# First heads' q and k at the head of the opening, row maxima of two groups taken ahead of a branch

## The chip, the cores and the metric

The kernel runs on one core of one Trainium2 chip. The metric is device time in microseconds of one execution, as the median of the runs shown. The engines are named as the profile names them: PE (TensorE matmul), PEld (its weight loads), DVE (VectorE), ACT (ScalarE), POOL (GpSimd) and SP (SyncE, which here only issues DMAs). Each engine works through its own instructions in program order and waits on semaphores for the others.

## The reference, cut to what matters

A transformer layer in float32 on x of shape (16, 512, 512): attention with 32 heads of 16, rotary embedding and a causal mask, then a gated feed-forward layer whose weights take the values -1, 0 and 1, each inside a layer norm on both sides, with residuals.

```python
h = _layernorm(x)
q, k, v = (split_heads(h @ W.T + b) for W, b in ((Wq, bq), (Wk, bk), (Wv, bv)))
q, k = (apply_rope(apply_rope(t, freqs_abs), freqs_temp) for t in (q, k))
s = jnp.where(causal, einsum('bhqd,bhkd->bhqk', q, k) / sqrt(dh), -inf)
out = einsum('bhqk,bhkd->bhqd', softmax(s), v) @ Wo.T + bo
x = x + _layernorm(out)
f = _layernorm(x)                     # gate_w, up_w (1408, 512), down_w (512, 1408)
x = x + _layernorm(((silu(f @ gate_w.T * gate_s) * (f @ up_w.T * up_s)) @ down_w.T) * down_s)
```

## The kernel before, in words

**Tiles and batches.** The 16 sequences ("batches") are worked one after the other. A batch has 512 rows in four blocks of 128 (`NB`), 512 features in four chunks of 128 (`NC`), and its 32 heads form eight groups of four (`NG`). The products q, k, v and o are float32 matmuls of 128x128 by 128x512; four of them, one for each chunk, make a block.

**Attention in steps.** A group takes six steps (`STEPS`), a pair of its heads at a third of the score matrix at a time. In one step (`one_step`, line 792) TensorE computes transposed scores of group n into the PSUM tile `st` (with the row maximum subtracted by a matmul of `mx` with ones), ACT takes their exponential into `pt`, POOL masks the diagonal; and scores of the group that follows into two PSUM tiles `s`, of which DVE takes row maxima (`maxima`, line 607). Steps 0 and 1 of group n take the maxima of group n + 1's last third, steps 2 to 5 those of group n + 2's first two. After step 2 `turn_maxima` (line 617) transposes a group's maxima, splits them into a high and a low part (`nmh`, `nml`) and has SP put them into rows of `mx`. A group's operands come from DRAM (`load_group`, line 549): q, and the high and low part of k (`kh`, `kl`), 256 KB each, three buffers of each. The weighted values (`values`, `av`) follow in steps 3 and 0.

**Filling.** Beside a step, TensorE works on a list of other matmuls: the projections of the batch to come and the feed-forward layer of the batch before. `run_list` (line 696) cuts such a list into as many equal shares of its costs as there are steps (1 for a float32 matmul of 512 columns, 0.15 for a transpose) and gives out one share for a step, behind the step's scores. A list item can be the issue of a DMA, of cost 0. The first list (`first_list`, line 884) holds what is left of batch 1's v, its q and k blocks, the transposes of batch 2's input and a product that folds biases: 46.4 units of cost. It is given out over 56 steps: ten that only take maxima (of group 0, and of group 1 but for its last third), ahead of group 0's own, and 46 of batch 0's 48.

**The q and k blocks** (`qk_block`, line 329). After the four matmuls into a PSUM tile, ACT makes two rotated copies (`ys`), DVE multiplies the PSUM tile by the cosines (`ya`), POOL multiplies `ys` by the sines; then (`rest`) DVE adds them into `ya`, ACT rounds it to a high part `yh`, POOL subtracts for a low part `yl`; then (`store`) SP writes both to DRAM in four DMAs. `ya` and `ys` have one buffer, `yh` and `yl` two. Projections, transposes and turned maxima share three PSUM buffers, taken in turn.

**The opening** (`front`, line 808). It loads x of batches 0 and 1, normalizes and transposes them, and computes batch 0's q (four blocks), k (four blocks) and v (four), and batch 1's first two v blocks, in this order. Each block's `rest` and `store` come after the first two matmuls of the next q or k block. Between the blocks it checks the feed-forward weights (`check_weights`, line 196): a copy on ACT rounds a weight tile, a DVE instruction compares it with the tile and counts what differs; 11 gate/up tiles of 512 KB and 11 down tiles of 256 KB, gate/up first. A last matmul sums the counts into `flag`. `run` (line 929) reads the flag on every engine and branches: the exact arm uses the weights in a format of fewer bits, the other in float32. Each arm holds all sixteen batches (`batches`, line 951). The arm that the inputs lead to is the exact one. Tiles filled ahead of the branch aren't carried into an arm, save those in fixed buffers; q, k and batch 1's normalized x are taken from DRAM.

Line 49 of the profile is a helper that keeps instructions in program order (class `InOrder`); nearly all instructions have that line, so groups are told apart by tile names.

Of the kernel before, what the change touches and what calls it, by code (L numbers as in the profile page):

```python
# [10 lines left out]
FP = mybir.dt.float32  # L11
FR = mybir.dt.float32r
# [6 lines left out]
P = 128  # L19
T = 512  # L20
# [4 lines left out]
NB = T // P  # L25
# [28 lines left out]
class Block:  # L54
# [55 lines left out]
    def constants(self):  # L110
        nc, a, con = self.nc, self.a, self.const
        for tb in range(NB):
            self.load_x(0, tb, ("x", "xr")[tb // 2], 2)
        ncol = sum(n for _, n in a["cols"][1])
        cols = con.tile([P, ncol], FP, tag="cols", name="cols")
        self.sp.dma_start(out=cols, in_=a["cols"][0])
        self.col, at = {}, 0
        for name, n in a["cols"][1]:
            self.col[name] = cols[:, at : at + n]
            at += n  # L120
        turn = con.tile([P, 2, T], FP, tag="turn", name="turn")
        self.cos, self.sin = turn[:, 0, :], turn[:, 1, :]
        nc.scalar.dma_start(out=turn, in_=a["turn"])
        for half in range(2):
            self.load_w(0, "q", half)
        for tb in range(NB):
            self.load_x(1, tb, "x1", 4)
        for half in range(2):
            self.load_w(0, "k", half)
        self.ident = con.tile([P, P], FP, tag="ident", name="ident")  # L130
        make_identity(nc, self.ident)
        self.neghalf = con.tile([P, 1], FP, tag="neghalf", name="neghalf")
        nc.gpsimd.memset(self.neghalf, -0.5)
        self.row = {}
        for name in ("bo", "dscale"):
            self.row[name] = con.tile([P, C], FP, tag=name, name=name)
            nc.scalar.dma_start(out=self.row[name], in_=a[name].partition_broadcast(P))

        self.gh = con.tile([P, self.NF], FP, tag="gh", name="gh")
        self.gu = con.tile([P, self.NF], FP, tag="gu", name="gu")  # L140

        self.mask = con.tile([P, T], mybir.dt.bfloat16, tag="mask", name="mask")
        nc.gpsimd.memset(self.mask, 0.0)
        m = self.mask[:, T - P : T]
        nc.gpsimd.affine_select(
            out=m, in_=m, compare_op=ALU.is_ge, fill=-BIG, base=0, pattern=[[-1, P]], channel_multiplier=1
        )
        self.v17 = []
        for i in range(2):
            t = con.tile([P, NB, WIDTH], FP, tag=f"v17_{i}", name=f"v17_{i}")  # L150
            nc.gpsimd.memset(t, 0.0)
            nc.gpsimd.memset(t[:, :, DH : H * W : W], 1.0)
            self.v17.append(t)
        self.one = con.tile([P, P], FR, tag="one", name="one")
        nc.vector.memset(self.one.bitcast(FP), 1.0)
        self.qd, self.kd, self.od, self.rd = [], [], [], []
        for par in range(2):
            for c in range(NC):
                self.qd.append(self.dram.tile([P, 2, T], FP, tag=f"qd{par}{c}", name="qd"))
                self.kd.append(self.dram.tile([2, P, T], FP, tag=f"kd{par}{c}", name="kd"))  # L160
                self.od.append(self.dram.tile([8 * 32, T], FP, tag=f"od{par}{c}", name="od"))
                self.rd.append(self.dram.tile([8, T], FP, tag=f"rd{par}{c}", name="rd"))
        self.wgs = self.dram.tile([self.NF, P, 2, NC, P], FP, tag="wgs", name="wgs")
        self.wds = self.dram.tile([self.F, C], FP, tag="wds", name="wds")
        self.wd = con.tile([P, self.NF, C], FR, tag="wd", name="wd")
        self.xn1 = self.dram.tile([P, NC, T], FP, tag="xn1", name="xn1")
        self.odd = con.tile([P, 2 * self.NF], FP, tag="odd", name="odd")
        self.flag = con.tile([1, 1], mybir.dt.int32, tag="flag", name="flag")
        self.ones = con.tile([P, 1], FP, tag="ones", name="ones")
        nc.vector.memset(self.ones, 1.0)  # L170


    def load_checks(self):

        a, n = self.a, 2 * NC * P
        ht = self.tile([P, self.NF, T], "ht", bufs=1).rearrange("p f t -> p (f t)")
        xl = self.tile([P, NC, T], "xntfl", bufs=1).rearrange("p c t -> p (c t)")
        places = [ht[:, ts(i, n)] for i in range(self.NF * T // n)] + [xl[:, ts(i, n)] for i in range(NC * T // n)]
        small = [tag for tag, k in (("oc", 4), ("q2", 3), ("kh", 3), ("kl", 3)) for _ in range(k)]
        self.wgu0, self.wd0 = [], []  # L180

        def load(f):
            w = places.pop() if 3 <= f < self.NF - 1 else self.tile([P, n], "wf", bufs=3)
            self.sp.dma_start(out=w, in_=a["wgu"][f].rearrange("p w c j -> p (w c j)"))
            self.wgu0.append(w)

        for f in range(self.NF - 1):
            load(f)
        for f in range(self.NF):
            tag = small.pop()  # L190
            w = self.tile([P, C], tag, bufs=4 if tag == "oc" else 3)
            self.sp.dma_start(out=w, in_=a["wd"][ts(f, P), :])
            self.wd0.append(w)
        self.load_last = lambda: load(self.NF - 1)

    def check_weights(self):
# [20 lines left out]
            self.pe.matmul(p[0:1, 0:1], n, self.ones, start=True, stop=True)  # L217
            self.dve.tensor_copy(self.flag, p[0:1, 0:1])

        return [lambda f=f, g=g: g(f) for g in (gate_up, down) for f in range(self.NF)] + [total]  # L220

    def load_x(self, b, tb, tag="x", bufs=2):
        t = self.tile([P, C], tag, bufs=bufs)
# [338 lines left out]
    def scores(self, n, m, i):  # L562
# [4 lines left out]
        if 0 <= n < self.B * NG:  # L567
            ps = self.ps_t.tile([P, 2, T], FP, tag="st", name="st")
            q, ks, mx = self.qs[n], self.ks[n], self.mxs[n]
            for j in range(2):  # L570
# [3 lines left out]
                for kb, at, w in ST_SETS[third]:  # L574
# [3 lines left out]
                        (out, ks[1][r, ts(kb, P)], x, False, False),  # L578
                        (out, self.one[r2, :], mx[r2, T - w : T], False, True),
                    ]  # L580
        if 0 <= m < self.B * NG:
            if n < 0 and i % 2:
                both = self.ps_t.tile([P, 2, T], FP, tag="st", name="st")
                pm = [both[:, j, :] for j in range(2)]
# [29 lines left out]
                accum_out=self.nms[m][:, j, qb : qb + 1],  # L614
            )

    def turn_maxima(self, m):
        p = self.psum("pm")
        self.pe.transpose(p[0:16, 0:P], self.nms.pop(m).rearrange("p j b -> p (j b)"), self.ident)
        hi, lo = [self.tile([16, P], i, bufs=1, dtype=FR) for i in ("nmh", "nml")]  # L620
        self.act.copy(hi, p[0:16, 0:P])
        self.dve.tensor_tensor(lo, p[0:16, 0:P], hi, ALU.subtract)
        mx = self.mxs[m] = self.tile([P, T], "mx", bufs=2, dtype=FR)

        def put():
            for i, t in enumerate((hi, lo)):
                self.sp.dma_start(out=mx[i:P:32, :].bitcast(FP), in_=t.bitcast(FP))

        self.later(1, put)
# [162 lines left out]
    def one_step(self, work, n, i):  # L792
        for f, args in self.todo.pop(self.step, []):
            f(*args)
        if i == 0 and n + 2 < self.B * NG:
            self.load_group(n + 2)
        self.scores(n, n + 2 if i >= 2 else n + 1, i)
        if i == 2 and 0 <= n + 1 < self.B * NG:
            self.turn_maxima(n + 1)
        next(work, None)  # L800
        if i == 3 and 0 <= n < self.B * NG:
# [6 lines left out]
    def front(self):  # L808
# [5 lines left out]
        def check(n):  # L814
            for _ in range(min(n, len(checks) - 1)):
                checks.pop(0)()
# [24 lines left out]
            rest = now  # L841
        rest()
        turn(0, NB - 1)
        for k in range(2):
            r = [norm(1, 2 * k), norm(1, 2 * k + 1)]
            check(1)
            for f in r:
                f()
        rests = []
        for name in "qk":  # L850
            for c in range(NC):
                items, rest, store = self.qk_block(0, name, c)
                for _, f in items[:2]:
                    f()
                for f in rests:
                    f()
                for _, f in items[2:]:
                    f()
                rests = [rest, store]
                if name == "q" and c < 2:  # L860
                    for k in range(2):
                        turn(1, 2 * c + k)
                check(2)
            if name == "q":
                for half in range(2):
                    self.load_w(0, "v", half)
            else:
                self.sp.dma_start(out=self.xn1, in_=self.xnts["a", 1])
        for f in rests:
            f()  # L870
        check(len(checks))
        nc.vector.tensor_scalar_mul(self.gh, self.col["gs"], 0.5)
        nc.vector.tensor_tensor(self.gu, self.gh, self.col["us"], ALU.mult)
        for tb in range(NB):
            for _, f in self.v_block(0, tb):
                f()
            if tb == 2:
                checks.pop(0)()
        self.wts[1, "v", 0], self.wts[1, "v", 1] = self.wts[0, "v", 0], self.wts[0, "v", 1]
        for tb in range(2):  # L880
            for _, f in self.v_block(1, tb):
                f()

    def first_list(self):

# [64 lines left out]

    def batches(self):
        B = self.B
        work = self.run_list(self.first_list(), 56)
        self.load_group(0)
        for n, i0 in ((-2, 2), (-1, 0)):
            for i in range(i0, STEPS):
                self.one_step(work, n, i)
        for b in range(B):
            if b:
                if b < B - 1:  # L960
# [78 lines left out]
```

## Time and profile before

| | |
|---|---|
| runs (us) | 3213.71, 3211.56, 3219.57; median 3213.71 |
| profiled execution, its own time | 3215.86 us |
| its span | 3214.0 us |
| mean granted TensorE clock | 0.984 |
| busy: PE, DVE, ACT, POOL | 3097.9, 1888.0, 1542.7, 1383.9 us |
| first TensorE instruction | at 10.38 us |
| batch 0's first scores for weights | at 108.42 us |
| moved by DMA | 471.41 MB, 147 GB/s over the span |

Times within the span are in microseconds from its start. A row of the timeline gives start, duration, engine, line, operation, output tile, inputs, shapes and count, and in brackets how long the engine had been idle before it and what ended the wait. A float32 matmul of 512 columns appears as two records. A row of busy times by stretch gives the stretch and its length, then for PE, PEld, DVE, ACT and POOL the busy time with the number of instructions, and last the granted clock of TensorE (1.00 is full), the DMA engines' busy share and GB/s. A row of waits gives who waited for whom, the total, the number of times and the longest.

### The profile page before, as it was taken

How to read it: one execution, taken by the hardware profiler on the slowest of the kernel's cores; microseconds unless marked ns; L12 is line 12 of the kernel's file. 1: busy time of each engine (PE TensorE's matmuls, PEld its weight loads, DVE VectorE, ACT ScalarE, POOL GpSimd, SP SyncE). 2: the span in 40 equal slices, each digit the busy share in tenths (PEclk: the TensorE clock that was granted, in tenths of full speed). 3: DMA queues.
4: the chain of work that ended last, by engine and by line, in shares of the span. 5: the costliest groups of instructions: out<-in, count | busy, mean ns of one | idle time of the engine just before them, and what ended most of it. 6: DMA issues, size and time to landing. Idle time of an engine off the chain costs nothing.

```text
span 3214.0 us, 59287 instructions
## 1 busy us (share of the span) xinstructions
PE 3097.9 (96%) x21258; PEld 1743.3 (54%) x21258; DVE 1888.0 (59%) x5911; ACT 1542.7 (48%) x2243; POOL 1383.9 (43%) x1933
## 2 busy tenths in 40 slices
PE   6889999999999999999999999999999999999988
PEld 2334555646556464655646455464655646455556
DVE  5465656556565665656566565665656566565633
ACT  5354545454554544545454554544455454453432
POOL 4143445443544534345443544534345453443343
PEclk9899999999999999999999999999999999999999
DMA  6454534445353443525345352543535345343422
GB/s 251 166 166 152 189 101 163 139 149 172 108 190 106 160 164 123 195 93 177 127 152 173 127 185 96 168 147 123 195 101 183 122 147 172 123 156 105 131 97 71
DMA packets 227441, 471.41 MB, mean 147 GB/s; under 512 B 40976, under 2 KB 45072, under 8 KB 226704
## 3 DMA queue, kind: packets, MB, share of 16 engines
q1 hardware_dynamic: 226704, 466.47, 43.1%
q8 instruction: 170, 2.79, 0.4%
q10 hardware_dynamic: 432, 1.05, 0.1%
q14 instruction: 135, 1.11, 0.1%
HBM read 345.79 MB, written 125.30 MB: 147 GB/s over the span
## 4 chain that ended last, share of the span: by engine, by line
PE 83%; DVE 2%; DMA 2%; ACT 2%; POOL 1%; issue 1%; SPq 0%; ACTq 0%; DVEq 0%; POOLq 0%
PE st L49 16%; PE pu L49 11%; PE pg L49 10%; PE av L49 9%; PE pd L49 9%; PE po L49 7%; PE pq L49 6%; PE pv L49 5%; PE pk L49 5%; PE s L49 3%; DMA kl<-kd 2%; PE px L49 1%; ACT pt L49 1%; DVE s L49 1%; PE pm L49 1%
## 5 line engine op out<-in xcount | busy, mean ns | idle before, releaser
L49 DVE CUSTOM_DVE_ANT_0 s<-s,mask 128x512 f32<-128x512 f32 (+1 forms) x2034 | 974.9, 510 | 713.8 <-PE s L49 530.8
L49 ACT ACTIVATE pt<-st 128x1024 f32<-128x1024 f32 (+1 forms) x768 | 677.0, 882 | 755.9 <-PE st L49 746.9
L49 POOL TENSOR_SCALAR_AFFINE_SELECT pt<-pt 128x256 f32<-128x256 f32 (+1 forms) x768 | 393.8, 513 | 1202.3 <-ACT pt L49 1200.0
L49 PEld LDWEIGHTS st<-q,kh 32*128 32x128 f32 x2048 | 191.3, 183 | 463.3 <-issue 225.6
L49 PE MATMUL st<-q,kh 32*128 32x512 f32 (+3 forms) x2048 | 411.2, 398 | 22.3 <-ACT pt L49 20.9
L49 PE MATMUL s<-kh,q 32*128 32x512 f32 (+1 forms) x2034 | 411.6, 399 | 17.2 <-DVE nm L49 8.8
L49 PE MATMUL s<-kl,q 32*128 32x512 f32 (+1 forms) x2034 | 340.7, 321 | 11.2 <-DMA kl<-kd 11.2
L49 PE MATMUL av<-pt,v 128*32 128x512 f32 (+3 forms) x4096 | 336.0, 447 | 0.0
L49 PE MATMUL st<-q,kl 32*128 32x512 f32 (+3 forms) x2048 | 333.5, 322 | 0.0
L49 PE MATMUL st<-mx,one 2*128 2x512 f32 (+3 forms) x2048 | 333.0, 321 | 0.0
L49 POOL TENSOR_TENSOR hl<-ht,hh 128x512 fp32r<-128x512 f32 (+1 forms) x192 | 229.6, 1196 | 184.3 <-ACT hh L49 176.7
L49 PE MATMUL pd<-wd,hl 128*128 128x512 f32 x704 | 288.9, 410 | 9.2 <-POOL hl L49 9.2
L49 PE MATMUL pd<-wd,hh 128*128 128x512 f32 x704 | 290.9, 413 | 2.2 <-ACT hh L49 2.2
L49 DVE DVE_READ_ACCUMULATOR2_ANT nm<- 128x1 f32 x2048 | 288.8, 141 | 0.0
L49 PE MATMUL pg<-xntf,wf 128*128 128x512 f32 x704 | 287.4, 408 | 1.5 <-ACT xntf L49 1.5
L49 PE MATMUL pu<-xntfl,wf 128*128 128x512 f32 x704 | 284.3, 404 | 0.0
L49 PE MATMUL pu<-xntf,wf 128*128 128x512 f32 x704 | 283.9, 403 | 0.0
L49 PE MATMUL pg<-xntfl,wf 128*128 128x512 f32 x704 | 281.5, 400 | 0.6 <-DVE xntfl L49 0.6
L49 PE MATMUL po<-w,oc 128*128 128x512 f32 x512 | 244.6, 610 | 3.7 <-DMA w<-in_wo 3.7
L49 PE MATMUL pq<-xnta,w 128*128 128x512 f32 x480 | 237.6, 626 | 6.9 <-ACT xntf L49 6.3
L49 PE MATMUL pk<-xnta,w 128*128 128x512 f32 x480 | 238.3, 615 | 4.3 <-DVE ya L49 3.7
L49 POOL TENSOR_TENSOR yl<-ya,yh 128x512 fp32r<-128x512 f32 x128 | 163.3, 1276 | 169.4 <-ACT yh L49 169.4
(118 smaller groups left out, 5021.8 us busy)
## 6 DMA issues: line engine op xcount, KB each, us to landing
wf<-wgs SPq DMA_DIRECT2D x176, 512.0 KB
q<-qd SPq DMA_DIRECT2D x128, 256.0 KB
kh<-kd SPq DMA_DIRECT2D x128, 256.0 KB
kl<-kd SPq DMA_DIRECT2D x128, 256.0 KB
od<-ot SPq DMA_DIRECT2D x128, 256.0 KB
w<-in_wo SPq DMA_DIRECT2D x34, 512.0 KB
xr<-in_x SPq DMA_DIRECT2D x66, 256.0 KB
w<-in_wq SPq DMA_DIRECT2D x32, 512.0 KB
```

Source lines behind the costliest of these rows:

```text
L49: return self.tc.keep_in_program_order(f(*args, **kwargs))
```

## The change

- The opening's blocks of batch 0 come in the order q0, k0, q1, k1, q2, v0, k2, v1, q3, v2, k3, v3 in place of all q, all k, all v (`block` in `front`). The halves of q's and k's weights are loaded in alternation. Batch 1's normalizations and transposes go between the first blocks. `rest` and `store` of a block wait in a list `then` for the second matmul of the next block of any kind.
- The weight tiles' loads and checks take the down tiles first.
- Groups 0 and 1 are loaded in the opening. Group 0's six maxima steps follow the blocks q3, v2 and k3, two at a time; group 1's are put between the matmuls of batch 1's v blocks, behind the flag.
- `keep_maxima` transposes and splits a group's maxima and stores them in a new DRAM tensor `mxd`; `load_maxima` reads them into `mx` in the arm.
- In the arm the ten warm-up steps are gone: groups 0 and 1 are loaded with their maxima, then batch 0's 48 steps begin, and the first list is given out over these 48. Steps 0 to 5 of group 0 compute no scores for a group whose maxima are there: in steps 0 and 1 nothing for group 1, from step 2 group 2 as before.

```diff
@@ constants
-        for half in range(2):
-            self.load_w(0, "q", half)
+        for name in "qk":
+            self.load_w(0, name, 0)
         for tb in range(NB):
             self.load_x(1, tb, "x1", 4)
-        for half in range(2):
-            self.load_w(0, "k", half)
+        for name in "qk":
+            self.load_w(0, name, 1)
...
+        self.mxd = [self.dram.tile([2, 4, T], FP, tag=f"mxd{m}", name="mxd") for m in range(2)]
@@ check_weights
-        return [lambda f=f, g=g: g(f) for g in (gate_up, down) for f in range(self.NF)] + [total]
+        return [lambda f=f, g=g: g(f) for g in (down, gate_up) for f in range(self.NF)] + [total]
@@ maxima
+    def keep_maxima(self, m):
+
+        for i, t in enumerate(self.turned_maxima(m)):
+            self.sp.dma_start(out=self.mxd[m][i].rearrange("j (b t) -> (j b) t", t=P), in_=t.bitcast(FP))
+        del self.qs[m], self.ks[m]
+
+    def load_maxima(self, m):
+        mx = self.mxs[m] = self.tile([P, T], "mx", bufs=2, dtype=FR)
+        for i in range(2):
+            self.sp.dma_start(out=mx[i:P:32, :].bitcast(FP), in_=self.mxd[m][i])
+
+    def turned_maxima(self, m):
         p = self.psum("pm")
         self.pe.transpose(p[0:16, 0:P], self.nms.pop(m).rearrange("p j b -> p (j b)"), self.ident)
...
@@ one_step
-        self.scores(n, n + 2 if i >= 2 else n + 1, i)
-        if i == 2 and 0 <= n + 1 < self.B * NG:
+        m = n + 2 if i >= 2 else n + 1
+        self.scores(n, None if m in self.mxs else m, i)
+        if i == 2 and 0 <= n + 1 < self.B * NG and n + 1 not in self.mxs:
             self.turn_maxima(n + 1)
@@ front, the old loop over q and k blocks and the v blocks left out
+        then = []
+
+        def block(name, c, n=0, scores=()):
+
+            qk = name in "qk"
+            items, *left = self.qk_block(0, name, c) if qk else (self.v_block(*c),)
+            for k, (_, f) in enumerate(items):
                 f()
+                if k == 1:
+                    for f in then:
+                        f()
+                    then.clear()
+            then.extend(left)
+            for m, i in scores:
+                self.scores(-2, m, i)
+            check(n)
+
+        now = [norm(1, tb) for tb in range(2)]
+        then += now
+        block("q", 0, 2)
+        then += [norm(1, tb) for tb in range(2, NB)]
+        block("k", 0, 2)
+        for tb in range(2):
+            turn(1, tb)
+        block("q", 1, 2)
+        for tb in range(2, NB):
+            turn(1, tb)
+        self.load_w(0, "v", 0)
+        block("k", 1, 2)
+        self.load_w(0, "v", 1)
+        self.sp.dma_start(out=self.xn1, in_=self.xnts["a", 1])
+        block("q", 2, 2)
+        block("v", (0, 0), 2)
+        block("k", 2, 2)
+        then += [lambda m=m: self.load_group(m) for m in range(2)]
+        block("v", (0, 1), 2)
+        block("q", 3, 1, [(0, 0), (0, 1)])
+        block("v", (0, 2), 2, [(0, 2), (0, 3)])
+        block("k", 3, 1, [(0, 4), (0, 5)])
+        then += [lambda: check(len(checks)), lambda: self.keep_maxima(0)]
+        block("v", (0, 3))
...
+        i = 0
+        for tb in range(2):
+            for k, (_, f) in enumerate(self.v_block(1, tb)):
                 f()
+                if tb == 0 and k == 0:
+                    checks.pop(0)()
+                elif i < STEPS:
+                    self.scores(-2, 1, i)
+                    i += 1
+        self.keep_maxima(1)
@@ batches
-        work = self.run_list(self.first_list(), 56)
-        self.load_group(0)
-        for n, i0 in ((-2, 2), (-1, 0)):
-            for i in range(i0, STEPS):
-                self.one_step(work, n, i)
+        work = self.run_list(self.first_list(), NG * STEPS)
+        for m in range(2):
+            self.load_group(m)
+            self.load_maxima(m)
```

## The prediction

> **What bounds the kernel now.** I read the page's slices first, then busy time by stretch of the opening, then the timeline around the marks of the opening, and last TensorE's waits in it. The slices:
>
> ```profile
> PE   6889999999999999999999999999999999999988
> PEclk9899999999999999999999999999999999999999
> ```
>
> TensorE fills the span except at both ends, and the change touches only the first: slices of 80 us, so the first three and a bit. By stretch (us; busy time of each engine with its instructions, then granted clock, DMA share, GB/s):
>
> ```profile
> 61.80:80.00 18.20, 11.39 (x28) 4.59 (x28) 12.28 (x28) 11.15 (x20) 7.26 (x6) 1.00 0.46 163
> 80.00:92.00 12.00, 12.00 (x24) 4.91 (x24) 0.10 (x1) 1.17 (x2) 0.00 (x0) 0.86 0.70 253
> 92.00:108.40 16.40, 14.84 (x74) 6.25 (x73) 13.78 (x57) 1.49 (x4) 0.00 (x0) 1.00 0.24 91
> 108.40:116.85 8.45, 4.36 (x26) 1.82 (x27) 2.81 (x8) 2.58 (x3) 0.81 (x2) 0.91 0.86 321
> 116.85:140.00 23.15, 21.52 (x174) 9.71 (x174) 12.08 (x45) 11.02 (x16) 6.43 (x10) 0.89 0.40 135
> 140.00:258.30 118.30, 100.46 (x771) 43.01 (x771) 67.86 (x244) 55.04 (x78) 43.91 (x64) 0.84 0.49 163
> 258.30:450.00 191.70, 190.50 (x1332) 107.92 (x1332) 115.10 (x365) 93.96 (x137) 84.44 (x118) 0.99 0.44 147
> ```
>
> From 258.3 us, where the second batch begins, TensorE idles 1 us in 190 at full clock. In the first batch's steps (116.85 to 258.3) it idles 19.5 us and loses (1-0.89)x23.15 + (1-0.84)x118.3 = 21.5 us more to a lowered clock. The marks:
>
> ```profile
> 79.95 0.15 DVE L49 CAST flag<-pm 1x1 int32<-1x1 f32 x1 [0.37 <-PE pm L49]
> 81.14 0.33 SPq L49 DMA_DIRECT2D q<-qd  x1
> 92.04 0.33 PE L49 MATMUL s<-kh,q 32*128 32x128 f32 x2
> 108.42 0.50 PE L49 MATMUL st<-q,kh 32*128 32x512 f32 x2
> 116.85 0.47 PE L49 MATMUL s<-kh,q 32*128 32x128 f32 x2 [3.95 <-DMA kh<-kd]
> ```
>
> The flag is ready at 80.1, SP has branched by 81.1, and TensorE still has v blocks until 92.0: the branch and the loads behind it are free. Ten warm-up steps (92.0 to 108.4) give the maxima of group 0 and part of group 1; group 0's weights start at 108.4; step 2 of group 0 gets going at 116.85, after a wait for group 2's keys. What TensorE waits for from there to 258.3:
>
> ```profile
> PE st L49 <- ACT pt L49: 13.0, 14, 2.0
> PE s L49 <- DVE nm L49: 4.9, 13, 0.7
> ```
>
> Ahead of the branch the q and k blocks are a chain over four engines, one block at a time, since ya has one buffer:
>
> ```profile
> 61.39 0.75 DVE L49 SCALAR_TENSOR_TENSOR ya<-pk,cols,turn 128x512 f32<-128x512 f32 x1 [2.15 <-POOL yl L49]
> 62.06 1.20 DVE L49 SCALAR_TENSOR_TENSOR kl<-kl,wd 128x512 f32<-128x512 f32 x1
> 64.52 0.62 ACT L49 CAST yh<-ya 128x512 fp32r<-128x512 f32 x1 [2.06 <-DVE ya L49]
> 65.21 1.26 POOL L49 TENSOR_TENSOR yl<-ya,yh 128x512 fp32r<-128x512 f32 x1 [2.50 <-ACT yh L49]
> 66.64 0.75 DVE L49 SCALAR_TENSOR_TENSOR ya<-pk,cols,turn 128x512 f32<-128x512 f32 x1 [2.15 <-POOL yl L49]
> ```
>
> A block with two wd checks takes 5.25 us, TensorE only 3.43 (4 matmuls of 0.86; the last eight v matmuls ahead of 92 took 7.03).
>
> **What the Trainium skill says.** "TensorE: Matmul & The Clock Gate", Part 1: The HAM clock gate, has TensorE drop to half clock after an idle window of about 3.4 us and return after a busy one. The trace agrees: after 5 us of idling the q block at 27.7 took 5.9 us instead of 3.43, and after the 3.95 us wait the mean clock was 0.53 for 5 us. "SBUF — State Buffer", Who interferes with whom, has VectorE with two SBUF inputs and GpSimd exclude each other: the wd check at 62.06, under a GpSimd product, took 1.20, the next 0.68. "DMA: Bandwidth & Descriptors", Anatomy of one DMA, has semaphore waits sit on the issuing sequencer, so that what stands behind on SP waits too; the trace has SP held 9.5 us by one nmh.
>
> **The change, part by part.** TensorE's arithmetic stays the same; what moves is waiting and clock.
>
> *Removed:* ten warm-up steps, 16.4 us, and the two half steps for group 1 inside steps 0 and 1. Their 12 maxima steps go ahead of the flag and behind it, 12 x 0.63 = 7.5 us of TensorE (pitches 0.66, 0.77, 0.45) and 14 us of VectorE (512 columns 0.65, 384 0.48, 256 0.38, 128 0.24; four heads, two groups). The ten list matmuls that rode in them go into the first batch, whose list now has 48 steps in place of 56.
>
> *The front, block by block* (times of the ya product; durations from the rows above and their like: two rotations 1.38, wd cast 0.6, gate/up cast 1.04 and its check 1.15, v copy 0.58, normalization 0.8). q0 ends on TensorE at 21.8; ya 23.2. k0 32.1: between them stand two wd checks, two statistics (2.0), the addition, yh, two normalizations, two rotations. q1 40.1: its PSUM buffer is k0's, free at 32.8, so TensorE idles 26.0 to 32.8 and its matmuls then need 5.5 at half clock. k1 46.1, q2 51.4 (plain blocks), k2 58.8 (a v copy and a gate/up cast more), q3 67.8 (four gate/up casts). The load of group 0 stands on SP behind k2's stores, which wait for yl at 65.05: it is issued 66.3 to 68.1, lands at 70.3, and TensorE, done with q3 at 61.5, waits for it. VectorE is in order, so from 68.5 it waits too, and q3's addition behind it: k3 84.0. Then four maxima, a check, addition, yh, two casts and two checks: flag at 93.2, 13.1 us later than before. TensorE has seven v matmuls (6.0) and group 1's steps (3.8) left, 102.9 with the transpose; it idled 3.6 us ahead of them, so I add 1.8 for half clock: 104.7.
>
> *The branch.* Nothing covers it now. Transpose, cast, difference, two stores to DRAM, branch: +1.9, SP starts loading at 106.6. Queued ahead of the first list item's data are three groups of three loads and four small ones for the maxima; then xnta (1 MB) and two halves of v's weights. Thirteen issues of about 0.6 put xnta at +8, and by bytes 2.36 + 1.05 + 0.52 = 3.93 MB at 370 GB/s (3.1 MB issued from 105.4 landed at 116.8 in the trace, 2 us of it latency) are there at +13 to +14. TensorE does step 0's weights at +5, then stands before its first v matmul until +14 (120.6), and two v matmuls and two steps at half clock bring step 2 to +18.7: 125.3, against 116.85: **8.4 later.** If part of the data came early the bubble would be 10, not 14; if the queues run as slowly as 300 GB/s, 17.
>
> *The first batch's 46 further steps* took 258.3-116.85 = 141.4. Now: -3.4 (clock lost from 117 to 125, (0.47+0.21)x5; my 18.7 has it already), +7.3 (list matmuls: 44.5 of 46.4 units remain in place of 36, 0.86 each). The list gave 0.83 matmuls to a step, so about ten steps had none; it now gives 0.97 and leaves one or two. Waits in the steps without one (125.94, 140.6 to 143.5, 157 to 159, 164.9, 172 to 174, 181, 195.4, 211.6, 247.2, 257, 258.3) sum to 11.7: I take -11. The low clock after 143 (5.1 us lost in ten) and half of that after 240 follow those waits: -6.5. Sum 127.8, so the batch ends at 253.1 in place of 258.3: **5.2 us earlier.** From both sides: nothing of the 11 and 6.5 gained gives +12 in all, everything idle or slow gone gives 112 + 5 for the steps and -16.
>
> *Taken at nothing:* the order of the weight loads (all have landed by 36 us, at 400 GB/s, before their checks; without that a check would wait about 1 us), group 0's store of maxima (1.2 us of SP, cover as the check chain runs on), the statistics' earlier place. The q weights of the list now follow the od store on SP: at most 1.5 us, within the error. From the second batch on the program is the same.
>
> The profiled execution took 3215.9 with a span of 3214.0, 2.1 above the median 3213.7; I apply the difference of -5.3 to the median: **3208.4 us.** What a measurement can tell from no change is about 0.3%, 9.6 us; before's runs spread 8.
>
> **Rivals.** *Denser is also steady.* With nearly every step filled, the first batch runs like the second, at full clock: 46 steps in about 117, 16 us earlier, 3198. For: stretch 258 to 450. Against: its transposes (after 195, 216, 233) remain steps with little matmul work and waits of 1 to 2 us on the exponentials. *Filler is not absorbed (the other side).* Each added matmul lengthens its step because exponentials, not missing matmuls, set the pace: 141.4-3.4+7.3 = 145.3, end at 270.6, +12, 3226. It decides from where less than 5 of the 17.5 us come back. For: the two longest waits (1.90 and 2.03) lie in steps that had transposes. Against: filled steps in the trace (131.7 to 138.7) run 2.2 to 2.6 us without a wait. *A short bubble and front.* Group 0's load lands earlier or the 14 us are 9: another 8 gained, 3200. For: DMA reached 410 GB/s in the opening. Against: thirteen issues in a row on SP. That the change doesn't act is excluded: the arm taken copies wgs, and both arms use the new code.
>
> **Numbers.** Likeliest case 0.53 (own range 3202 to 3216), steady 0.22, unabsorbed 0.14, short bubble 0.11. Faster: most of the steady case, over half of the short bubble, little of the likeliest: 0.33. Slower: most of the unabsorbed and a long front: 0.14. Same 0.53. Range 3194 to 3224, which holds the error of a walked front (some 6 us) and both outer cases nearly whole.
>
> **What would show it.** The flag near 93 and group 0's first maxima near 70 confirm the front; TensorE idle near 8 to 9 us ahead of its first v matmul of the branch, waiting for xnta or w, confirms the bubble; waits on the exponentials in the first batch falling from 13 to under 5 us and its clock above 0.9 confirm the rest. A front done before 95, or steps of group 0 to 7 as slow as before (18.5 us a group), would make it wrong.

## The result and the profile after

The changed kernel takes 3239.3 us (median; 3233.5 to 3243.4) against 3216.6 (3211.0 to 3222.5) for the kernel before in the same comparison: ratio 1.0069, 95% interval 1.0051 to 1.0088, so 16 to 28 us more. The forecast was 3208.4 with a range to 3224. It was wrong in sign and outside its range. The profiled execution took 3243.4 us with a span of 3241.7, 27.7 more than the span before. It is the slowest of the six runs, 4.1 above their median, so its profile overstates the loss somewhat.

The slices of the kernel after:

```profile
PE   6789999999999999999999999999999999999988
PEclk8689999999999999999999999999999999999999
```

Only the opening differs from before (688 and 989 there): TensorE does less in the second slice, and its clock is lower in the first three. The same in stretches (us; busy time and instructions of PE, PEld, DVE, ACT, POOL, then granted clock, DMA share, GB/s):

```profile
95.00:110.00 15.00, 15.00 (x36) 5.44 (x36) 6.54 (x24) 0.59 (x1) 0.00 (x0) 0.50 0.02 7
...
120.00:135.00 15.00, 4.18 (x10) 1.60 (x10) 0.00 (x0) 1.02 (x1) 0.41 (x1) 0.50 0.68 243
135.00:147.00 12.00, 12.00 (x60) 4.95 (x56) 3.71 (x16) 3.65 (x4) 1.68 (x3) 0.50 0.00 1
...
138.00:290.00 152.00, 134.86 (x990) 57.45 (x993) 80.09 (x291) 68.00 (x95) 51.77 (x74) 0.84 0.49 166
...
288.93:481.00 192.07, 190.79 (x1354) 107.93 (x1352) 116.26 (x366) 95.35 (x139) 85.83 (x120) 1.00 0.44 148
```

From 95 to 110 TensorE is busy all the time, at half clock. From 120 to 135 it works 4 us of 15. From 135 to 147 it is again busy throughout, at half clock. The steps of the first batch (138 to 290) have the clock of before, 0.84, and idle 17 us. The second batch is as it should be. The marks, from the timeline:

```profile
95.12 2.08 PE L49 MATMUL pv<-w,xntf 128*128 128x512 f32 x2
95.23 0.15 DVE L49 CAST flag<-pm 1x1 int32<-1x1 f32 x1 [0.37 <-PE pm L49]
114.08 0.28 PE L49 MATMUL pm<-ident,nm 128*16 128x128 f32 x1
115.75 0.34 SPq L49 DMA_DIRECT2D q<-qd  x1
119.54 0.79 PE L49 MATMUL st<-q,kh 32*128 32x512 f32 x2 [5.18 <-DMA kh<-kd]
132.45 2.05 PE L49 MATMUL pv<-w,xnta 128*128 128x512 f32 x2 [10.77 <-DMA w<-in_wv]
```

The flag is there at 95.4, group 1's maxima are turned at 114.1, SP loads from 115.75, and TensorE then stands twice: for group 0's keys and for the weights of its first v matmul. A v matmul takes 2.08 us here; at 112.90, with the clock back, it takes 1.12. And what TensorE waits for from 138 to 290 (who, for whom, total, times, longest):

```profile
PE st L49 <- ACT pt L49: 5.7, 5, 2.1
PE st L49 <- DMA mx<-nml: 4.6, 1, 4.6
PE s L49 <- DVE nm L49: 2.4, 7, 0.6
PE pq L49 <- DMA w<-in_wq: 1.5, 1, 1.5
PE s L49 <- DMA kh<-kd: 1.3, 1, 1.3
```

The waits on exponentials fell from 13.0 to 5.7, though not to the forecast's "under 5"; three waits on DMAs came in their place, and the clock stayed at 0.84 where the forecast had it above 0.9. Against the forecast's own marks:

| | forecast | measured |
|---|---|---|
| flag ready | 93.2 | 95.4 |
| from there to group 1's turned maxima | 11.5 | 18.7 |
| to SP's first load in the arm | 1.9 | 1.7 |
| to the first v matmul of the arm | 14.0 | 16.7 |
| to step 2 of group 0 | 4.7 | 5.6 |
| step 2 of group 0 at | 125.3 | 138.0 |
| the 46 steps from there | 127.8 | 151.7 |

The second batch begins with group 8's first step, which issues the load of group 10: at 288.9 in place of 257.5, 31.4 us later. The end of the 46 steps in the table is put as much later than before's 258.3. From there to the load of group 18, eight groups on, the kernel after takes 192.4 us in place of 197.6, which gives five back. The forecast had nothing there; the five kernels below whose list is also given out over 48 steps took 192.0 to 193.0, the other seven 195.2 to 198.7, and why is not shown. The rest is scatter between executions.

### The profile page after: what moved, and what is told of

The parts are those of the page before. It is cut to its first block, busy times and chain, and to the rows that moved or that the text cites. A ratio compares the mean times of both kernels' runs of the same rounds, so it can differ in the third digit from the quotient of the medians.

```text
span 3241.7 us, 59284 instructions
## 1 busy us (share of the span) xinstructions
PE 3109.2 (96%) x21258; PEld 1746.0 (54%) x21258; DVE 1888.3 (58%) x5911; ACT 1542.5 (48%) x2243; POOL 1384.1 (43%) x1933
## 4 chain that ended last, share of the span: by engine, by line
PE 85%; DMA 4%; DVE 3%; ACT 2%; issue 1%; POOL 1%; SPq 1%; ACTq 0%; DVEq 0%; POOLq 0%
PE st L49 16%; PE pu L49 11%; PE pg L49 10%; PE av L49 9%; PE pd L49 9%; PE po L49 7%; PE pq L49 7%; PE pv L49 6%; PE pk L49 6%; PE s L49 3%; DMA kl<-kd 2%; PE px L49 1%; SPq L49 1%; DVE s L49 1%; ACT pt L49 1%
## 5 line engine op out<-in xcount | busy, mean ns | idle before, releaser
L49 DVE CUSTOM_DVE_ANT_0 s<-s,mask 128x128 f32<-128x128 f32 (+1 forms) x2032 | 973.7, 510 | 739.1 <-PE s L49 550.8
L49 PE MATMUL s<-kh,q 32*128 32x128 f32 (+1 forms) x2032 | 410.6, 399 | 18.1 <-DMA kh<-kd 11.4
L49 PE MATMUL s<-kl,q 32*128 32x128 f32 (+1 forms) x2032 | 340.3, 322 | 13.1 <-DMA kl<-kd 13.0
L49 PE MATMUL pv<-w,xnta 128*128 128x512 f32 x464 | 235.4, 640 | 12.7 <-DMA w<-in_wv 12.7
## 6 DMA issues: line engine op xcount, KB each, us to landing
q<-qd SPq DMA_DIRECT2D x130, 256.0 KB
kh<-kd SPq DMA_DIRECT2D x130, 256.0 KB
kl<-kd SPq DMA_DIRECT2D x130, 256.0 KB
od<-ot SPq DMA_DIRECT2D x128, 256.0 KB
xr<-in_x SPq DMA_DIRECT2D x66, 256.0 KB
```

What stands on the lines that cost most here:

```text
L49: return self.tc.keep_in_program_order(f(*args, **kwargs))
```

## The experiments

Theory: the loss has three parts, a half clock behind the flag, a gap behind the branch that nothing covers, and list matmuls that the first batch doesn't absorb. The rivals put it into the new order of the blocks alone, or into the maxima alone. All ratios are to the kernel before on the same chip; "batch 1" stands for the issue of group 10's load in the profile (257.5 before, 288.9 after).

| run | batch 1 at | ratio, 95% interval |
|---|---|---|
| after | 288.9 | 1.0069 [1.0051, 1.0088] |
| e1, fill at the flag | 275.4 | 1.0062 [1.0043, 1.0081] |
| e2, dense matmuls first | 284.6 | 1.0068 [1.0048, 1.0088] |
| e3, loads in order of need | 283.6 | 1.0054 [1.0034, 1.0074] |
| e4, order alone | 263.9 | 1.0028 [1.0017, 1.0040] |
| e5, maxima alone | 301.2 | 1.0105 [1.0085, 1.0124] |
| e6, gap filled | 268.1 | 1.0043 [1.0023, 1.0062] |
| e10, group 0 only | 268.7 | 1.0012 [0.9998, 1.0027] |
| e11, group 0 and fills | 262.5 | 1.0036 [1.0025, 1.0047] |
| e9, before, group 2 early | 256.0 | 0.9977 [0.9965, 0.9990] |
| e12, before, steps filled | 251.3 | 1.0000 [0.9988, 1.0012] |
| e13, before, nine tiny | 256.4 | 1.0005 [0.9994, 1.0016] |
| e14, before, forty tiny | 270.3 | 1.0045 [1.0028, 1.0062] |

**e1: is it the clock behind the flag?** Five unread matmuls (nothing uses their results) keep TensorE busy while it waits for the sum of the flag.

```diff
@@ front, batch 1's first v block, behind its first matmul
+                    fill = self.ps_av.tile([P, T], FP, tag="av", name="av")
+                    for _ in range(5):
+                        self.pe.matmul(fill, self.xnts["a", 1][:, 0, 0:P], self.wts[1, "v", 0][:, 0, :], start=True, stop=True)
                     checks.pop(0)()
```

> The changed kernel with five matmuls more (128x128 by 128x512, results unused, into the PSUM tile that only values use later) in TensorE's wait for the flag (91.6 to 95.0 us). Clock theory: group 1's maxima steps behind the flag ran at half clock from 95 to 111 because TensorE had idled 2.3 and 3.4 us just before; with the gap filled they run at full clock, and the stretch from the flag to the turned maxima of group 1 falls from 18.8 us to about 11.5, the kernel by about 6 us (3233 from 3239), though TensorE does more work. Pace theory: VectorE's maxima and the two PSUM tiles set the pace there; the stretch stays near 19 us and the kernel gains nothing or loses the 1 us by which the flag is later.

From the flag (96.4) to the turned maxima (107.4), a stretch of e1:

```profile
96.39:107.40 11.01, 10.95 (x47) 4.08 (x46) 8.40 (x32) 0.63 (x2) 0.00 (x0) 1.00 0.01 3
```

The same matmuls take 11.0 us at full clock in place of 18.7: 7.7 us of that stretch were clock. In the profile batch 1 begins 13.5 us earlier; the time fell by about 2 us, which these runs can tell neither from nothing nor from the 6 expected.

**e2: dense v matmuls ahead of group 1's steps.**

```diff
-                elif i < STEPS:
-                    self.scores(-2, 1, i)
-                    i += 1
+        for i in range(STEPS):
+            self.scores(-2, 1, i)
```

> The changed kernel with batch 1's seven remaining v matmuls back to back behind the flag, and group 1's six maxima steps after them, in place of one between each two. Clock theory: the dense matmuls bring the clock back within about 4 us, so that the steps run at full clock and are paced by VectorE (7.5 us): turned maxima about 3 to 4 us earlier. Pace theory: the maxima no longer overlap with the v matmuls, so the stretch grows to 6 + 7.5 + the same slowness, 3 us or more later.

Behind the flag (97.6) in stretches of e2:

```profile
97.00:103.00 6.00, 5.75 (x11) 2.52 (x12) 0.25 (x3) 0.59 (x1) 0.00 (x0) 0.72 0.08 24
103.00:109.00 6.00, 4.24 (x24) 1.83 (x22) 2.93 (x10) 0.59 (x1) 0.00 (x0) 1.00 0.00 0
109.00:115.00 6.00, 2.85 (x17) 1.52 (x17) 5.24 (x24) 0.00 (x0) 0.00 (x0) 0.67 0.00 1
```

The dense matmuls do bring the clock back, but six maxima steps in a row are then bound by VectorE (5.24 of 6 us), TensorE idles and the clock falls again. The maxima are turned at 114.6, 17.0 us behind the flag, only 1.7 less than after and less than expected; the time doesn't change.

**e3: the arm's loads in the order in which TensorE needs them.**

```diff
@@ batches; the list loses the loads of x and v's weights that come here
-        for m in range(2):
-            self.load_group(m)
-            self.load_maxima(m)
+        self.load_group(0)
+        self.load_maxima(0)
+        self.load_xn1()
+        for half in range(2):
+            self.load_w(1, "v", half)
+        self.load_group(1)
+        self.load_maxima(1)
```

> The changed kernel with the arm's first loads in the order in which they are needed: group 0, its maxima, batch 1's normalized x and v's weights, then group 1, its maxima, group 2. Queue theory: 3.9 MB stood ahead of v's weights and TensorE idled 5.2 and 10.8 us for them; with 2.4 MB ahead the first v matmul comes about 9 us behind SP's first load in place of 16.7, and the kernel gains about 7 us. Rival: the gap is latency of stores, branch and a first load, not queued bytes; then less than 2 us are gained.

The arm's first v matmul in the timeline of e3:

```profile
127.28 2.04 PE L49 MATMUL pv<-w,xnta 128*128 128x512 f32 x2 [3.91 <-DMA w<-in_wv]
```

It comes 10.3 us after SP's first load (116.94) in place of 16.7: 6.4 us of the gap were the loads of groups 1 and 2 ahead in SP's queue, 1.57 MB. The other 10 go to group 0's loads, to the data of the v matmul itself and to latency, which this run doesn't separate. The mean clock stayed at 0.52 to 145, and batch 1 began 5.4 us earlier; the time fell by about 5 us, inside the interval.

**e4 and e5: the order alone, the maxima alone.** e4 has the new block order, loads and checks, but group 0's loads, the maxima and the 56 steps of the list as before. e5 has the old order, with both groups' maxima taken between its v blocks and kept.

```diff
@@ e4, against the kernel after
-        block("q", 3, 1, [(0, 0), (0, 1)])
+        block("q", 3, 1)
...
-        work = self.run_list(self.first_list(), NG * STEPS)
-        for m in range(2):
-            self.load_group(m)
-            self.load_maxima(m)
+        work = self.run_list(self.first_list(), 56)
+        self.load_group(0)
+        for n, i0 in ((-2, 2), (-1, 0)):
+            for i in range(i0, STEPS):
+                self.one_step(work, n, i)
@@ e5, v blocks with maxima between their matmuls, against the kernel after
+        todo = [(m, i) for m in range(2) for i in range(STEPS)]
...
+                elif tb >= 2 and todo:
+                    m, i = todo.pop(0)
+                    self.scores(-2, m, i)
+                    if i == STEPS - 1 and m == 0:
+                        self.keep_maxima(0)
```

> The new block order, weight order and check order alone: no maxima ahead of the branch, the ten warm-up steps and the list over 56 steps as before. If the maxima's move is what costs: flag near 84.5 us in place of 95.3 (and 80.1 before), branch covered by the v matmuls behind it, kernel within 4 us of before (about 3220). If the new order of blocks is what costs: flag above 90 us and the kernel 10 us or more above before.

> The maxima's move alone: block order, weight order and check order as before; groups 0 and 1 are loaded behind the last k block's stores, their twelve maxima steps go between the matmuls of the v blocks from the third on, both groups' maxima are kept in DRAM, and the arm is that of the changed kernel. If the move is what costs: flag at 80 us as before, then 15 v matmuls and 12 steps, mostly at half clock since TensorE had waited for the flag (up to 110 us; 101 at full clock), a gap of 16 to 17 us behind SP's first load, kernel 12 to 18 us above before. If the order of blocks was the larger part: kernel within 5 us of before.

The wait ahead of the flag in the timeline of e4:

```profile
84.61 0.19 PE L49 MATMUL pm<-ones,odd_sum 128*1 128x1 f32 x2 [7.62 <-DVE odd_sum L49]
```

The flag comes at 85.0, five later than before, and TensorE has run dry 7.6 us ahead of it; most of the steps behind it run at half clock (0.50 from 100 to 112). The order alone costs 9 us (5 to 13): its mark fell where the first reading put it, its time nearly where the second did. e5 costs 34 us, nearly twice the most that was expected. The two don't add up to the loss of the kernel after (43 against 23 us), so neither can be read as a share of it. Stretches of e5:

```profile
80.00:100.00 20.00, 17.85 (x44) 6.45 (x42) 7.62 (x28) 0.59 (x1) 0.00 (x0) 0.50 0.22 78
100.00:122.00 22.00, 20.88 (x51) 8.01 (x50) 9.87 (x37) 1.44 (x3) 0.00 (x0) 0.53 0.01 1
```

Half clock for 42 us in a TensorE that is 92% busy: v matmuls one at a time between 32-row score matmuls didn't bring the clock back in all that time (two waits of TensorE, 2.15 and 1.12 us, lie in it). In the kernel before twelve v matmuls ran in a row from 80 to 92, and the clock was back within about 4 us:

```profile
80.00:84.00 4.00, 4.00 (x7) 1.67 (x8) 0.10 (x1) 0.00 (x0) 0.00 (x0) 0.64 0.50 161
84.00:92.00 8.00, 8.00 (x19) 3.24 (x17) 0.00 (x0) 1.17 (x2) 0.00 (x0) 0.96 0.80 299
```

**e6: e1, e3 and eleven unread matmuls in the gap behind the branch.**

```diff
@@ the list, ahead of batch 1's v blocks; six more ahead of the branch
+        do(self.fill, 5)
         for tb in range(2, NB):
             L += self.v_block(1, tb)
```

> The changed kernel with the fill of the flag's wait, the arm's loads in the order of need, and 11 matmuls of no use more in the gap at the branch (6 ahead of it, 5 behind step 0's scores). Clock theory: the loss behind the gap (steps at half clock for some 17 us, about 8 us lost) goes too, on top of 6.7 us from the flag's wait and 6.4 us from the loads: group 10 is loaded near 268 us against 288.9, the kernel near 3219. Rival (the clock comes back late because of the steps' own idle time, not the gap): 275 us and 3226.

A stretch of e6:

```profile
110.00:135.00 25.00, 23.24 (x120) 9.64 (x118) 6.37 (x27) 6.50 (x8) 2.90 (x6) 0.93 0.55 194
```

From 135 to 160 the clock is 1.00. Batch 1 begins at 268.1, where the first reading put it: queue and clock together account for 20.8 of the 31.4 us in the profile. The time fell by 8 or 9 us only, in place of some 20; what profile and time can say of each other is taken up under e12.

**e10: only group 0's maxima ahead of the branch.** Group 1's stay in the arm, in four warm-up steps, and so only seven v matmuls of batch 1 stand between flag and arm on TensorE.

```diff
-        then += [lambda m=m: self.load_group(m) for m in range(2)]
+        then += [lambda: self.load_group(0)]
...
+        self.load_group(0)
+        self.load_maxima(0)
+        self.load_group(1)
+        for i in range(2, STEPS):
+            self.one_step(work, -1, i)
```

> The changed kernel with group 1's maxima left in the arm as before: four steps that only take maxima, then group 0's; the list over 50 steps; only group 0's maxima are kept. Branch theory: the flag's branch is now covered by seven v matmuls, SP loads from 97 us while TensorE works until 104, the gap shrinks from 16 to about 4 us, and the kernel comes to about 3222. Rival (the first list's data would be late anyway, and the gap only moves): no more than 5 us gained.

SP loads at 97.5, one microsecond behind the flag; TensorE waits 5.5 us for loads at the branch in place of 16 (about 4 expected), and batch 1 begins 20 us earlier than after. The ratio can't be told from no change: 18 of the 23 us are gone, in time and not only in a profile. So what costs most is the chain of group 1's maxima between flag and branch.

**e11: e10 with unread matmuls** (five at the flag, three and four in the arm) and group 2's load two steps ahead of group 0's first.

```diff
+            if i == 2:
+                self.fill(3)
+            if i == 4:
+                self.load_group(2)
             self.one_step(work, -1, i)
```

> The changed kernel with only group 0's maxima taken ahead of the branch, five unread matmuls ahead of the sum of the flag, three ahead of the first warm-up step in the arm and four behind it, and group 2's load two steps before group 0's first. By the clock theory TensorE then stays at full clock from 95 to 130, where the same kernel without them lost some 14 us, and batch 1 begins 10 to 14 us earlier than there, at 255 to 259: 3211 to 3216, faster than the kernel before by 0.1 to 0.3%. If the low clock there cost nothing because loads set the pace, batch 1 begins at 265 or later and the time is that of the kernel before or 3 us more.

The clock was 1.00 from 95 to 115, but 2.9 us of waits for loads were left of e10's 5.5, and it fell again at 115 (0.60 to 120); batch 1 began at 262.5, between the two expectations, and the time was no better than e10's: 1.0036. The expected gain is refuted.

**e9: the kernel before with group 2 loaded in the second warm-up step,** so that step 2 of group 0 doesn't wait 3.95 us for its keys.

```diff
+        if n == -1 and i == 1:
+            self.load_group(2)
-        if i == 0 and n + 2 < self.B * NG:
+        if i == 0 and n + 2 < self.B * NG and n != 0:
             self.load_group(n + 2)
```

> The kernel before with one edit: group 2 is loaded at the first warm-up steps, behind group 1, and not at group 0's step 0 behind 2 MB of other loads. If the wait of 3.95 us at 112.6 and the half clock behind it are a matter of SP's queue: both go, 5 to 7 us less than before. If other bytes take their place: no change.

The wait is gone, and the kernel is faster than before by 3 to 11 us (0.9977), as the first reading had it. It beats both. In the profile batch 1 begins only 1.5 us earlier, since a lower clock took the rest (0.73 from 120 to 145 and 0.66 to 170, before 0.91 and 0.77), so where the gain lies is not shown.

**e12: the forecast's step on the first batch by itself.** The kernel before, with one unread matmul in each of nine steps that had none.

```diff
+            if filled and s >= 10 and done - begun < 0.5:
+                self.fill(1)
             yield
```

> The kernel before, with one matmul of 512 columns whose result nobody reads in each of the nine steps of the first batch that had no matmul from the list. Nothing else changes, so this is the step of the prediction on the first batch by itself. If such a matmul is absorbed by the waits of its step and keeps the clock up, as predicted (11 us of waits and 6.5 us of low clock gone for 7.7 us of matmuls), batch 1 begins near 248 in place of 257.5 and the kernel is 10 us faster. If the exponentials set the pace and the clock doesn't follow, batch 1 begins near 265 and the kernel is 8 us slower. Between 254 and 259 half of it is absorbed.

TensorE's waits of e12 from 127 to 258 (11.5 and 4.9 before, from the same stretch):

```profile
PE st L49 <- ACT pt L49: 5.9, 7, 1.9
PE s L49 <- DVE nm L49: 5.2, 14, 0.7
```

The stretch of e12 between the loads of groups 3 and 10 (before's stands in the next section):

```profile
127.65:251.32 123.67, 110.77 (x896) 48.12 (x897) 74.49 (x266) 61.82 (x87) 48.02 (x69) 0.93 0.50 166
```

With nine matmuls (7.7 us) more, batch 1 begins at 251.3, 6.2 us earlier: 14 of the forecast's 17.5 us do come back when nothing but matmuls is added, some 5 of waits and the rest of clock (0.93 in place of 0.86). Four kernels with the same steps and list (before, e4, e13, e14) took 129.8 to 130.5 us in this stretch, so its 123.7 is hardly scatter. Yet the time is that of before, within 4 us.

From group 10's load to the end the span is 2965 us in e12 (2966 in e6 and e11), against 2956.5 before and 2952.8 after, with the same program from there on. Added matmuls, which the expectation of e13 makes the mark of the long ones, are not that mark: e4 has none and took 2963, e1 has five and took 2956. The fourteen profiles, one of each kernel, lie between 2949 (e3) and 2966 us in this stretch, and a kernel's own runs spread by 20 us (before: 3208 to 3229 next to e12). So 9 us in single profiles prove nothing here, and that e12 as a rule runs longer behind its first batch is not shown. **e13 and e14** put nine and forty tiny unread matmuls into an idle stretch of the opening, to see whether the place of TensorE's instructions in the program does that.

```diff
@@ e13; range(40) in e14
+        av = self.ps_av.tile([P, T], FP, tag="av", name="av")
+        for _ in range(9):
+            self.pe.matmul(av[:, 0:16], self.ident, self.ident[:, 0:16], start=True, stop=True)
```

> The kernel before with nine unread matmuls of 16 columns while TensorE idles for its first q block (22 to 27 us). They cost no time where they stand. The three kernels with nine or more added matmuls ran 9 us longer behind their first batch than all the others, with the same instructions and the same waits there. If that comes from where TensorE's later instructions stand in the program, this kernel too takes 8 to 10 us more from batch 1 on and is 0.25 to 0.3% slower than the kernel before. If it comes from how the first batch ran, it takes the time of the kernel before, within 2 us.

> The same with forty of these matmuls, still inside the idle time. By position, the time from batch 1 on changes by some other amount, between 0 and 10 us more than before. By the other reading, as before within 2 us.

e13 takes 1.6 us more than before by its ratio (-2 to +5), not the 8 to 10 of the first reading; its 2960 us from group 10's load to the end lie within the scatter. e14 was badly sized. Its forty matmuls didn't fit into the idle time, its first ya came at 40.0 in place of 27.0 and batch 1 12.8 us later, which is most of its 14.5; behind batch 1's start it took 2957.5, as before. Position is not supported. Why e12's median shows none of the 6.2 us stays open.

## Why the prediction was wrong

**Right.** The front up to q3's ya was walked to within 0.3 us (67.53 against 67.8), the q1 block's wait for k0's PSUM buffer included (6.62 us measured, 6.8 forecast), and the flag to 2.2. The branch took 1.7 for 1.9. That nothing covers the branch any longer was right, and so was the direction of the waits on exponentials.

**"So I add 1.8 for half clock: 104.7."** This step failed. The forecast took the clock to return within one busy window, from the Trainium skill, "TensorE: Matmul & The Clock Gate", Part 1: The HAM clock gate, which puts the return after about 3.4 us of sustained work. The trace doesn't agree for this mix: 15.0 us of 15.0 busy at 0.50. Without this term the forecast had 9.7 us for the stretch; it took 18.7, and e1 shows that 7.7 of the 9.0 are clock. The same thing happened first, and smaller, behind the wait for group 0's keys (timeline of the kernel after):

```profile
73.58 5.80 PE L49 MATMUL pv<-w,xnta 128*128 128x512 f32 x8
```

Four v matmuls took 5.80 us in place of 3.43, after waits of 7.05 and 0.63 us; VectorE then stood 2.39 us for the scores behind them, and k3's ya came 2.2 us late (86.2 against 84.0), as the flag did. The walk had no half clock there.

**"until +14 (120.6)".** Measured 16.7, within the forecast's own bounds of 10 and 17. The rate was sized too high: 3.93 MB at 370 GB/s, while the 3.1 MB and 9.4 us from which that rate was read make 330, and e3's 1.57 MB for 6.4 us are 245 (estimates).

**"two v matmuls and two steps at half clock".** The half clock was in the sum, but only to 125; it held to 147, nine us behind step 2.

**"I take -11" and "follow those waits: -6.5".** Neither came. This is the largest part of the miss, 17.5 of the 36.6 us by which batch 1 began later than forecast. Between the loads of groups 3 and 10, in the kernel before and in the kernel after:

```profile
127.22:257.49 130.27, 112.41 (x874) 47.95 (x871) 73.79 (x262) 61.32 (x86) 47.42 (x68) 0.86 0.49 162
...
150.64:288.93 138.29, 121.15 (x903) 51.31 (x901) 75.50 (x271) 64.77 (x91) 50.09 (x71) 0.86 0.53 182
```

Idle time went from 17.9 to 17.1, the clock's loss from 18.2 to 19.4 (an estimate from the mean clock), and work grew by the remaining 7.6 (forecast 7.3). A group took 19.8 us on average over the 46 steps, where the forecast named 18.5 as a sign of being wrong. That is the rival "Filler is not absorbed", which had 0.14, and more than it: 151.7 us against its 145.3. Its reason wasn't the rival's, though. The waits on ACT and DVE fell by half, from 16.4 to 8.1; 7.6 us of waits on DMAs came in, the largest for group maxima, in SP's queue and then on TensorE (timeline of the kernel after):

```profile
220.96 0.33 SPq L49 DMA_DIRECT2D rd<-sum  x1
226.19 0.64 SPq L49 DMA_DIRECT2D xr<-rd  x1
226.87 0.60 SPq L49 DMA_DIRECT2D mx<-nmh  x1
...
230.45 0.80 PE L49 MATMUL st<-mx,one 2*128 2x512 f32 x2 [4.60 <-DMA mx<-nml]
```

xr is read from rd, so its issue waits 4.9 us for rd's store to land, and mx stands behind it. Both belong to attention's own output, not to the list; the list's part is what stood ahead of rd: four stores of q and a load of x in the 4 us before it, 0.75 MB. In the kernel before the same rd (at 193.54) had only the load of x in the 4 us ahead of it, 0.25 MB, and xr waited 2.7 us. It is the place that the forecast cited from the skill, "DMA: Bandwidth & Descriptors", Anatomy of one DMA: a wait sits on the issuing sequencer. The forecast had the rule and used it for the arm's first loads; in the list it priced the q weights alone ("at most 1.5 us", which is what they took), as nothing.

The runs on record bear this out in part. The wait for mx is 3.4 to 4.6 us in all six kernels that give the list out over 48 steps (after, e1, e2, e3, e5, e6), 2.0 in e10 and none in e11 with 50 steps, and none in before, e4, e9 and e12 with 56. The stretch between the loads of groups 3 and 10 took 134 to 140 us in the first six and 127 to 129 with 50 steps. So the loss comes with the denser list, and e12 shows that bare matmuls are absorbed. That the DMAs are what keeps the real items from being absorbed is read from these waits, and no run took one DMA away.

**The range.** The errors before step 2 (12.7 us) and after it (23.9) have one sign, and a low clock has a part in both: 7.7 us behind the flag by e1, and in the steps a loss that grew by 1.2 where 6.5 were to go. The range treated them as separate cases and ended at 3224, below the 3226 at which the unabsorbed rival alone stood. Two smaller readings were off and change little: the q block at 27.7 held TensorE for 6.4 us, not 5.9, and the mean clock in the 5 us from 116.85 was 0.50, not 0.53.

## What to carry to other kernels

Before moving work ahead of a branch or a load, write down what TensorE does while they pass: the old order had twelve us of dense matmuls there, and both the cover and the clock hung on them. Where a step is to be filled with list items, count the DMAs that come with them in the queue that also feeds the step (here the likely cause, not one shown). A gain in one stage of one profile is no gain in time until the medians show it: here batch 1 began 6 us earlier in one kernel with no change of its time, and the same later work took from 2949 to 2966 us in fourteen profiles.

## What the hardware showed that was not expected

- A TensorE without a gap can stay at half clock: 15 us and more in the kernel after (95 to 110), and 42 us at 92% busy in e5, with single 512-column matmuls between 32-row ones. A like mix held full clock in the kernel before (92 to 108) and in e1 (96.4 to 107.4), where dense matmuls came first.
- Dense matmuls brought the clock back within some 4 us (before from 80; e2 from 97, 0.72 in the first 6 us and 1.00 in the next). The mix took about 17 us for it in the kernel after, from 95 to 112 and from 132 to 149. What makes the difference is not shown.
- The clock fell behind a wait of 1.48 us (kernel after: 0.99 from 150 to 160, and the 512-column matmul behind the wait, at 160.04, took 2.07 us).
- Unread matmuls can shorten a stretch: with five of them in the wait for the flag, the stretch behind it took 7.7 us less.
- Fourteen profiles with the same program from batch 1 on differed there by up to 17 us (2949 to 2966). The cause is open.
